# Local transformer on Trainium2: transposing the probabilities one step later, ahead of the feed-forward pieces

## The chip, the cores and the metric

The kernel runs on one core of one Trainium2 chip. The metric is device time in microseconds (us) of one execution. Five engines work side by side, each through its own list of instructions in order: TensorE (PE: matmuls and transposes; PEld is its loading of weights), VectorE (DVE), ScalarE (ACT), GpSimd (POOL), and SyncE (SP), which here only issues DMAs. An engine whose next instruction has to wait lets everything behind it wait too.

## The reference, cut to what matters

The program has two blocks. The part touched here is the second half of block 0: six layers of a local transformer over 16 sequences of 256 tokens with 128 features, in float32.

```python
def attn_layer(x, Wqkv, qs, ksc, Wo):        # 16 heads of 64 features
    q, k, v = split(x @ Wqkv)
    q, k = l2norm(q) * qs, l2norm(k) * ksc
    q, k = rotary(q), rotary(k)              # with rotate_half
    out = local_attention(q, k, v)           # windows of 32 queries, 64 keys: own window and the one before
    return out @ Wo

def ffn_layer(x, g, bln, W1, b1, W2, b2):
    xn = layernorm(x) * g + bln
    a, gate = split(xn @ W1 + b1)
    return a * gelu(gate) @ W2 + b2

for i in range(6):
    x = attn_layer(shift_tokens(x), ...) + x
    x = ffn_layer(shift_tokens(x), ...) + x
```

Before it stands one other attention with its feed-forward, after it a third attention and a last feed-forward; the change touches neither.

## The kernel before

**Tiling.** The 16 sequences are 8 units `u` of two sequences (128 features on the partitions, 512 tokens). The state of a unit lies in `zs[u]`. The 1024 columns of q and k are 8 parts of 128 (two heads each). One step `n` of the main loop takes two parts of one unit; 4 steps (`QS`) are a unit, 32 steps (`per`) a layer, `N` = 192 steps all six layers. "n mod 4" below is the place of a step in this round of four; every unit has one feed-forward, so a round of four steps also holds one feed-forward.

**The pipeline.** All engines but SP are in the order of the program text (`manual_schedule`); the order of SP's DMAs is chosen by the framework's planner. A step works on several stages of different parts at once:

- `project` (step n): q and k of two parts (L705), ACT squares them (L708), DVE makes the two terms of the rotary embedding (L710, L713), four DMAs per part swap halves (`got<-sent`).
- `rotate` (n-1): POOL adds the swapped term (four instructions, L721). `norms_sum` (L729), `norms_inverse` (L747 and small POOL operations) and `norms_rows` (L781) find the inverse norms of two steps at a time, the first two in even steps, the last in odd ones; `widened` fetches them back by DMA (`kn<-rkh`).
- `scaled` (n-4, the head of the step): POOL multiplies k by its norm (two instructions, L802). Then `scores` (L858), `maxima` (DVE, L870 and L872), `exponentials` (ACT, L880: 16 activations, half of them for each of the two parts x), `divided` (DVE reciprocal L893, POOL multiplication L895, once for each x).
- `flipped` (n-5): four transposes (L903) for each x and a copy of the result out of PSUM into `prT`, by ACT for x = 0 (L911), by DVE for x = 1 (L909).
- `weighted` (n-8): the probabilities times the windows of the state (L921), copied into `zx` by DVE and ACT (L934, L936). A unit's first `weighted` needs the last `flipped` of that unit, which stands earlier in the same step.
- `merging` (n-9): `zx` times the merged value and output weights (L942); after four of them `add_to_state` (L955).

`upright` (L809, L813) and `windows` write a unit's state to DRAM and fetch its windows, once or twice per unit.

**The feed-forward** is a generator, `ffn`, in 15 pieces. It is queued in `behind` in the step that ends its unit's `merging`, and `go_on(behind)` runs one piece of it at four places of a step. In this document these are called A (near the head of the step), B (after `weighted`), C (after `norms_inverse`, before `project`) and D (inside `project`). Piece 1 takes the mean (L968) and piece 2 the squares, at C and D of the step that queues it. Piece 3, at A of the next step, sums the squares (L977), takes a power on POOL (`rs`, L987) and widens it on POOL (`fs`, L989). Piece 5, at C of that same step, transposes `fs` (L994) and normalises (L995, L996). Piece 7, at A of the next step, is the gates (L1004) with their gelus on ACT (L1006), piece 11 the other half (L1014, L1018), piece 15 the last product (L1027) with its addition to the state (L957).

**PSUM.** Four banks `mm` go round among all users in program order, three banks `sim` hold scores, one holds `y`. A user of a bank waits until the result of four users before has been copied out.

Of the kernel before, what the change touches and what calls it, by code (L numbers as in the profile page):

```python
# [21 lines left out]
DEPTH = 6  # L22
INNER = 1024
NP = INNER // 128
# [20 lines left out]
def adaln_kernel(  # L45
# [5 lines left out]
    nc = tc.nc  # L51
# [186 lines left out]
    with block:  # L238
# [19 lines left out]
        pt = bank()  # L258
# [341 lines left out]
    with ExitStack() as es:  # L600
# [8 lines left out]
        def atile(tag, shape, bufs=None):  # L609
            kw = {} if bufs is None else {"bufs": bufs}  # L610
            return at.tile(list(shape), F32, tag=tag, name=tag, **kw)
# [166 lines left out]
        def norms_rows(rk):  # L778

            pt = bank()  # L780
            nc.tensor.transpose(pt[0:32, 0:128], rk.rearrange("p t e -> p (t e)"), ident)  # L781
            rows = small("rkT", (32, 128), 2)
            nc.scalar.copy(rows, pt[0:32, 0:128])
            home = dk.tile([8, 4, 128], F32, tag="rkh", name="rkh")
            nc.sync.dma_start(home.rearrange("e t p -> t e p"), rows)
            return home
# [104 lines left out]
        def divided(pr, ssum):  # L891
            rsum = small("rsum", (128, 8))
            nc.vector.reciprocal(rsum, ssum.rearrange("p t h -> p (t h)"))  # L893
            prf = pr.rearrange("p t h k -> p (t h) k")
            nc.gpsimd.tensor_tensor(  # L895
                prf, prf, rsum.unsqueeze(2).to_broadcast([128, 8, 64]), ALU.mult
            )

        def flipped(p, x, pr, prT):

            pt = bank()
            for st in range(4):
                nc.tensor.transpose(  # L903
                    pt[:, st * 128 : (st + 1) * 128],
                    pr[:, x, st].rearrange("p h k -> p (h k)"),
                    ident,
                )
            if x:
                nc.vector.tensor_copy(prT[:, p + x, :], pt)  # L909
            else:  # L910
                nc.scalar.copy(prT[:, p + x, :], pt)  # L911

        def weighted(j, xw, prT):

            zx = atile("zx", (128, 2, NP, 128))
            for k in (2 * j, 2 * j + 1):
                pz = [bank(), bank()]
                for w in range(2):
                    for par in range(2):
                        r = slice(64 * par, 64 * par + 64)  # L920
                        nc.tensor.matmul(  # L921
                            pz[par][:, w * 256 : (w + 1) * 256],
                            xw[r, (2 * k + w) % 8, :],
                            prT[r, :, 64 * k + 32 * w : 64 * k + 32 * w + 32],
                            start=True,
                            stop=True,
                            skip_group_check=True,
                        )
                for par in range(2):
                    c0 = 64 * (k % 2)  # L930
                    dst = zx[:, par, :, c0 : c0 + 64].rearrange("p a (w q) -> p w a q", w=2)
                    src = pz[par].rearrange("p (w a q) -> p w a q", w=2, a=NP)
                    if par:
                        nc.vector.tensor_copy(dst, src)  # L934
                    else:
                        nc.scalar.copy(dst, src)  # L936
            return zx
# [99 lines left out]
        QS = NP // 2  # L1037
        per = NU * QS
        N = DEPTH * per
# [3 lines left out]
        qs, squares, got, prs, prTs = {}, {}, {}, {}, {}  # L1043
# [3 lines left out]
        behind, merges = [], []  # L1047

        def place(n):

            return n // per, n % per // QS, 2 * (n % QS)
# [5 lines left out]
        def go_on(parts):  # L1057
            for g in list(parts):
                if next(g, parts) is parts:
                    parts.remove(g)  # L1060
# [1 line left out]
        es.enter_context(tc.manual_schedule(engines=ENGINES))  # L1062
        merges.append(merged(0))
        n = 0
        while n < N + 9 or behind:
            layer, at_ = divmod(n, per)
            if at_ == 13 and 0 < layer < DEPTH:
                wffs[layer] = load_ffn(layer)
            if 0 <= n - 4 < N:
                for m in (2 * (n - 4), 2 * (n - 4) + 1):  # L1070
                    scaled(m, kns.pop(m))

            w, j = divmod(n - 9, QS)
            if 0 <= w < DEPTH * NU:
                if j == 0:
                    pys[w] = psy.tile([128, 512], F32, tag="y", name="y")
                merging(j, zxs.pop((w, j)), vos[w // NU], pys[w])
                if j == QS - 1:
                    add_to_state(w % NU, pys.pop(w))
            if n % 2 and 3 <= n <= N + 1:  # L1080
                home = norms_rows(rk)
            go_on(behind)
            go_on(merges)
            if 0 <= n - 1 < N:
                for m in (2 * (n - 1), 2 * (n - 1) + 1):
                    rotate(m, qs[m], got.pop(m))
            if 0 <= n - 5 < N:
                i, u, p = place(n - 5)
                if p == 0:
                    prTs[i, u] = atile("prT", (128, NP, 512))  # L1090
                flipped(p, 0, prs[n - 5], prTs[i, u])
            for s, lag in ((0, 7), (1, 9)):
                v, r = divmod(n - lag, QS)
                if r == 0 and 0 <= v < DEPTH * NU:
                    if s == 0:
                        upright(v % NU, rows[v % 2])
                    xws[v, s] = windows(s, rows[v % 2])
            if 0 <= n - 5 < N:
                flipped(p, 1, prs.pop(n - 5), prTs[i, u])
            if 0 <= n - 3 < N:  # L1100
                masked()
            sims = banks[2 * (n - 4) : 2 * (n - 3)] if 0 <= n - 4 < N else None

            if n % 2 == 0 and 2 <= n <= N:
                n2 = norms_sum([squares.pop(m) for m in range(2 * n - 4, 2 * n)])
            v, r = divmod(n - 8, QS)
            if 0 <= v < DEPTH * NU:
                zxs[v, r] = weighted(r, xws[v, r // 2], prTs[v // NU, v % NU])
            go_on(behind)
            if sims:  # L1110
                m = 2 * (n - 4)
                rn = inverses[m // 4][:, m % 4 // 2]
                scores(sims, m, [qs.pop(m), qs.pop(m + 1)])
                pr = atile("pr", (128, 2, 4, 2, 64), 1)
                nbs = [maxima(sims[par], rn[:, par]) for par in range(2)]
                ssum = small("ssum", (128, 2, 4, 2))

            if n % 2 == 0 and 2 <= n <= N:
                rk, inverses[n // 2 - 1] = norms_inverse(n2)
            if 0 <= w < DEPTH * NU and j == QS - 1:  # L1120
                behind.append(ffn(w % NU, w // NU))
            go_on(behind)
            between = exponentials(0, sims, nbs, rn, pr, ssum) if sims else iter(())
            for m in (2 * n, 2 * n + 1):
                if n < N:
                    i, u, p = place(n)
                    qs[m], squares[m], got[m] = project(i, u, m, wqk[p + m % 2], between)
                if m % 2 == 0:
                    go_on(behind)
            if sims:  # L1130
                for x in range(2):
                    for _ in between:
                        pass
                    divided(pr[:, x], ssum[:, x])
                    between = exponentials(1, sims, nbs, rn, pr, ssum) if x == 0 else iter(())
                prs[n - 4] = pr
            if 0 <= n - 3 < N:
                masked()
                for m in (2 * (n - 3), 2 * (n - 3) + 1):
                    kns[m] = widened(m, home)  # L1140
            if layer + 1 < DEPTH:
                if at_ == 18:
                    merges.append(merged(layer + 1))
                if at_ > per - QS:
                    p = 2 * (at_ - (per - QS) - 1)
                    wqk[p : p + 2] = [load_qk(layer + 1, p), load_qk(layer + 1, p + 1)]
            if at_ == 0 and 0 < layer < DEPTH:
                wqk[NP - 2 :] = [load_qk(layer, NP - 2), load_qk(layer, NP - 1)]
            n += 1
# [4 lines left out]
    with ExitStack() as es:  # L1154
# [302 lines left out]
        N = NU * NP  # L1457
# [3 lines left out]
        prs, prTs, oTs, running = {}, {}, {}, []  # L1461
        n = 0
        while n <= N + 4 or running:
            u, p = divmod(n, NP)
            if n < N:
# [4 lines left out]
                sims = [scores(s, q, kT) for s in range(2)]  # L1470
            copies = []
            if 0 <= n - 1 < N:
                u1, p1 = divmod(n - 1, NP)
                g, j = divmod(p1, 4)
# [17 lines left out]
            for lag, g, s in ((6, 0, 0), (7, 0, 1), (9, 1, 0), (10, 1, 1)):  # L1492
                v, r = divmod(n - lag, NP)
# [7 lines left out]
            v, r = divmod(n - 10, NP)  # L1501
# [116 lines left out]
```

## Time and profile before

| | |
|---|---|
| median of 3 runs | 4238.45 us (4237.72 to 4245.77) |
| the profiled execution, its own time | 4247.72 us |
| its span | 4245.9 us |
| TensorE busy | 3844.1 us, 91% of the span |
| DVE, ACT, POOL busy | 2840.9, 2924.1, 2660.5 us (67%, 69%, 63%) |
| mean granted TensorE clock | 0.974 |
| `project` of the first step to that of the last | 268 us to 3540 us after the start of the span |

Busy time of TensorE is time in which at least one matmul is on its way; a granted clock of 1 is full speed, and it is either 1 or 0.5 at any moment. Idle time of an engine that isn't the bound costs nothing. Views used below: the list of waits (engine, line, what it waited for; total us, times, longest us) and the timeline (start in us, duration in us, engine, line, operation, result and inputs, shape, count, and in brackets the idle time before it and what ended it).

### The profile page before, as it was taken

How to read it: one execution, taken by the hardware profiler on the slowest of the kernel's cores; microseconds unless marked ns; L12 is line 12 of the kernel's file. 1: busy time of each engine (PE TensorE's matmuls, PEld its weight loads, DVE VectorE, ACT ScalarE, POOL GpSimd, SP SyncE). 2: the span in 40 equal slices, each digit the busy share in tenths (PEclk: the TensorE clock that was granted, in tenths of full speed). 3: DMA queues.
4: the chain of work that ended last, by engine and by line, in shares of the span. 5: the costliest groups of instructions: out<-in, count | busy, mean ns of one | idle time of the engine just before them, and what ended most of it. 6: DMA issues, size and time to landing. Idle time of an engine off the chain costs nothing.

```text
span 4245.9 us, 117219 instructions
## 1 busy us (share of the span) xinstructions
PE 3844.1 (91%) x44534; PEld 2509.1 (59%) x44534; DVE 2840.9 (67%) x5910; ACT 2924.1 (69%) x9973; POOL 2660.5 (63%) x3374
## 2 busy tenths in 40 slices
PE   7867899999999999999999999999999998799998
PEld 4534666666666666666666666666666666555554
DVE  7745667676766767676766676666667675376664
ACT  4536777777777777777776777777777776366665
POOL 5446666766667676666676666767666665155453
PEclk9888999999999999999999999999999999899999
DMA  1334444444444444454444444444444443200000
GB/s 40 40 90 106 124 114 120 119 113 118 120 114 123 115 114 121 109 129 111 123 117 116 115 117 119 117 120 117 118 107 121 110 120 81 66 1 6 9 4 11
DMA packets 316618, 408.82 MB, mean 96 GB/s; under 512 B 48745, under 2 KB 212632, under 8 KB 316056
## 3 DMA queue, kind: packets, MB, share of 16 engines
q1 hardware_dynamic: 316056, 401.33, 37.8%
q8 instruction: 352, 5.77, 0.6%
q14 instruction: 210, 1.72, 0.1%
HBM read 178.26 MB, written 21.56 MB: 47 GB/s over the span
## 4 chain that ended last, share of the span: by engine, by line
PE 34%; ACT 30%; DVE 14%; issue 7%; POOL 6%; SPq 5%; DMA 4%; ACTq 0%; POOLq 0%; DVEq 0%
ACT pr L880 18%; PE mm L921 8%; PE sim L858 6%; ACT sq L708 6%; PE mm L903 3%; POOL pr L895 3%; PE mm L729 3%; DVE sent L710 3%; DVE mx L870 3%; DMA xw<-rows 3%; PE mm L1396 2%; SPq L793 2%; PE sim L1323 2%; DVE nb L872 2%; PE mm L1386 2%
## 5 line engine op out<-in xcount | busy, mean ns | idle before, releaser
L880 ACT ACTIVATE pr<-sim,nb,rq 128x64 f32<-128x64 f32 x3072 | 1226.6, 448 | 374.0 <-DVE nb L872 362.1
L895 POOL TENSOR_TENSOR pr<-pr,rsum 128x512 f32<-128x512 f32 x384 | 398.6, 1043 | 779.2 <-DVE rsum L893 723.9
L942 PEld LDWEIGHTS y<-zx,wvo 128*128 128x128 f32 x6144 | 715.7, 192 | 91.4 <-issue 88.5
L880 ACT ACTIVATION_READ_ACCUMULATOR pr<-sim,nb,rq 128x1 f32 x3072 | 762.3, 248 | 0.0
L705 PE MATMUL mm<-z,wqk 128*128 128x512 f32 x1536 | 715.7, 605 | 22.8 <-DVE fx L970 12.9
L942 PE MATMUL y<-zx,wvo 128*128 128x128 f32 x6144 | 717.5, 275 | 1.2 <-ACT zx L936 1.2
L710 DVE SCALAR_TENSOR_TENSOR sent<-mm,vec,rope 128x512 f32<-128x512 f32 x768 | 568.5, 740 | 109.8 <-ACT sq L708 101.4
L802 POOL TENSOR_TENSOR k<-k,kn 128x512 f32<-128x512 f32 x384 | 483.4, 1276 | 127.3 <-DMA kn<-rkh 117.5
L721 POOL TENSOR_TENSOR q<-q,got 128x512 f32<-128x512 f32 x384 | 489.1, 1274 | 13.9 <-DMA got<-sent 10.4
L721 POOL TENSOR_TENSOR k<-k,got 128x512 f32<-128x512 f32 x384 | 495.8, 1291 | 0.0
L708 ACT ACTIVATE sq<-mm 128x512 f32<-128x512 f32 x768 | 473.1, 616 | 21.1 <-PE mm L705 20.8
L705 PEld LDWEIGHTS mm<-z,wqk 128*128 128x128 f32 x1536 | 274.6, 191 | 351.0 <-issue 226.1
L934 DVE COPY zx<-mm 128x512 f32<-128x512 f32 x384 | 265.5, 691 | 295.5 <-PE mm L921 295.5
L903 PE MATMUL mm<-ident,pr 128*128 128x128 f32 x1536 | 253.8, 289 | 225.4 <-POOL pr L895 131.1
L921 PE MATMUL mm<-prT,xw 64*128 64x256 f32 x3072 | 424.4, 405 | 5.7 <-DVE zx L934 3.9
L921 PEld LDWEIGHTS mm<-prT,xw 64*128 64x128 f32 x3072 | 321.5, 195 | 127.4 <-issue 55.0
L903 PEld LDWEIGHTS mm<-ident,pr 128*128 128x128 f32 x1536 | 166.1, 144 | 374.0 <-POOL pr L895 358.6
L870 DVE TENSOR_REDUCE mx<-sim 128x8 f32<-128x512 f32 x384 | 263.2, 685 | 173.7 <-PE sim L858 173.6
L936 ACT COPY zx<-mm 128x512 f32<-128x512 f32 x384 | 225.2, 586 | 214.7 <-PE mm L921 214.7
L1366 POOL TENSOR_TENSOR pr<-pr,rsum 128x256 f32<-128x256 f32 (+1 forms) x256 | 205.4, 834 | 244.6 <-DVE rsum L1364 221.0
L858 PEld LDWEIGHTS sim<-k,q 64*32 64x32 f32 x24576 | 264.3, 106 | 90.2 <-issue 42.4
L858 PE MATMUL sim<-k,q 64*32 64x64 f32 x24576 | 300.3, 227 | 18.0 <-POOL k L802 10.6
(254 smaller groups left out, 6386.6 us busy)
## 6 DMA issues: line engine op xcount, KB each, us to landing
got<-sent SPq DMA_DIRECT2D x1536, 128.0 KB
kn<-rkh SPq DMA_DIRECT2D x768, 128.0 KB
xw<-rows SPq DMA_DIRECT2D x384, 128.0 KB
rows<-xt SPq DMA_DIRECT2D x96, 128.0 KB
wqk<-in_L_ffn_Wqkv_dram SPq DMA_DIRECT2D x48, 128.0 KB
bhome<-brow SPq DMA_DIRECT2D x1, 3072.0 KB
wv<-in_L_ffn_Wqkv_dram SPq DMA_DIRECT2D x12, 256.0 KB
wo<-in_L_ffn_Wo_dram SPq DMA_DIRECT2D x12, 256.0 KB
```

The lines of the kernel that those rows point to most:

```text
L705: nc.tensor.matmul(pp, wqk[:, j, :], xs, start=True, stop=True)
L708: nc.scalar.activation(sq, pp, AF.Square)
L710: nc.vector.scalar_tensor_tensor(two(sent[:, j, :]), two(pp), scale, tab[1], ALU.mult, ALU.mult)
L721: nc.gpsimd.tensor_tensor(r, r, two(got[:, j, :]), ALU.add)
L802: nc.gpsimd.tensor_tensor(k, k, two(kn), ALU.mult)
L858: nc.tensor.matmul(sims[par][32 * c : 32 * c + 32, c0 : c0 + 64], q[r, s, t0 : t0 + 32], k[r, s, t0 : t0 + 64], start=False, stop=True, sk ...
L870: nc.vector.tensor_reduce(mx, sim.rearrange("p (b k) -> p b k", b=8), AX.X, ALU.max)
L880: nc.scalar.activation(pr[:, x, st, par, :], sims[par][:, b * 64 : (b + 1) * 64], AF.Exp, bias=nbs[par][:, b : b + 1], scale=rn[:, par, b ...
L895: nc.gpsimd.tensor_tensor(prf, prf, rsum.unsqueeze(2).to_broadcast([128, 8, 64]), ALU.mult)
L903: nc.tensor.transpose(pt[:, st * 128 : (st + 1) * 128], pr[:, x, st].rearrange("p h k -> p (h k)"), ident,)
L921: nc.tensor.matmul(pz[par][:, w * 256 : (w + 1) * 256], xw[r, (2 * k + w) % 8, :], prT[r, :, 64 * k + 32 * w : 64 * k + 32 * w + 32], star ...
L942: nc.tensor.matmul(py[:, j * 128 : (j + 1) * 128], vo[:, h, :], zx[:, h % 2, h // 2, :], start=(h == 0), stop=(h == 2 * NP - 1), skip_grou ...
```

## The change

Six edits, all in the loop of the local transformer:

- The probabilities wait one step longer: `flipped` takes those of n-6 instead of n-5, and `weighted`, `merging`, `upright`, `windows` and the loading of the feed-forward's weights move one step with it. The loop has one step more.
- Both `flipped` of a step stand together; the copy of x = 0 goes from ACT to DVE.
- `rotate`, `flipped`, `upright` and `windows` now stand ahead of place A of the feed-forward, of the pieces of weight merging (`merges`) and of `norms_rows`.
- `divided` of x = 1 moves from the end of its step to the next step, behind the two `flipped` and ahead of place A.
- `pr`, the probabilities, gets two buffers instead of one.
- `zx`, the weighted state, gets one buffer instead of two.

```diff
@@ flipped
-            if x:
-                nc.vector.tensor_copy(prT[:, p + x, :], pt)
-            else:
-                nc.scalar.copy(prT[:, p + x, :], pt)
+            nc.vector.tensor_copy(prT[:, p + x, :], pt)
@@ weighted
-            zx = atile("zx", (128, 2, NP, 128))
+            zx = atile("zx", (128, 2, NP, 128), 1)
@@ the loop
-        while n < N + 9 or behind:
+        while n < N + 10 or behind:
             layer, at_ = divmod(n, per)
-            if at_ == 13 and 0 < layer < DEPTH:
+            if at_ == 14 and 0 < layer < DEPTH:
                 wffs[layer] = load_ffn(layer)
...
-            w, j = divmod(n - 9, QS)
+            w, j = divmod(n - 10, QS)
...
-            if n % 2 and 3 <= n <= N + 1:
-                home = norms_rows(rk)
-            go_on(behind)
-            go_on(merges)
             if 0 <= n - 1 < N:
                 for m in (2 * (n - 1), 2 * (n - 1) + 1):
                     rotate(m, qs[m], got.pop(m))
-            if 0 <= n - 5 < N:
-                i, u, p = place(n - 5)
+            if 0 <= n - 6 < N:
+                i, u, p = place(n - 6)
                 if p == 0:
                     prTs[i, u] = atile("prT", (128, NP, 512))
-                flipped(p, 0, prs[n - 5], prTs[i, u])
-            for s, lag in ((0, 7), (1, 9)):
+                pr = prs.pop(n - 6)
+                for x in range(2):
+                    flipped(p, x, pr, prTs[i, u])
+            if 0 <= n - 5 < N:
+                divided(prs[n - 5][:, 1], ssum[:, 1])
+            for s, lag in ((0, 8), (1, 10)):
                 v, r = divmod(n - lag, QS)
...
-            if 0 <= n - 5 < N:
-                flipped(p, 1, prs.pop(n - 5), prTs[i, u])
+            go_on(behind)
+            go_on(merges)
+            if n % 2 and 3 <= n <= N + 1:
+                home = norms_rows(rk)
...
-            v, r = divmod(n - 8, QS)
+            v, r = divmod(n - 9, QS)
...
-                pr = atile("pr", (128, 2, 4, 2, 64), 1)
+                pr = atile("pr", (128, 2, 4, 2, 64), 2)
...
             if sims:
-                for x in range(2):
-                    for _ in between:
-                        pass
-                    divided(pr[:, x], ssum[:, x])
-                    between = exponentials(1, sims, nbs, rn, pr, ssum) if x == 0 else iter(())
+                for _ in between:
+                    pass
+                divided(pr[:, 0], ssum[:, 0])
+                for _ in exponentials(1, sims, nbs, rn, pr, ssum):
+                    pass
                 prs[n - 4] = pr
```

## The prediction

> **What bounds the kernel now.** The page first: which engine is fullest.
>
> ```profile
> PE 3844.1 (91%) x44534; PEld 2509.1 (59%) x44534; DVE 2840.9 (67%) x5910; ACT 2924.1 (69%) x9973; POOL 2660.5 (63%) x3374
> ```
>
> TensorE. Between 480 and 3560 us it is covered for 2854.71 of 3080 us. Rounds of four steps are 69.1 us long (mean of 41, scores to scores), so TensorE lacks 225.3 / 3080 x 69.1 = 5.05 us a round: all that a better order could win. The list of waits says on what:
>
> ```profile
> PEld mm L903 <- POOL pr L895: 358.6, 312, 6.3
> PE mm L903 <- POOL pr L895: 131.1, 178, 5.5
> PE mm L903 <- ACT fg L1006: 47.2, 46, 2.8
> ```
>
> Mostly the transposes wait for the divided probabilities; `PEld` overlaps matmuls, the `PE` rows are real gaps. Next, TensorE through one step, from scores of an n = 0 (mod 4) step to those of the next:
>
> ```profile
> 2104.97 1.48 PE L858 MATMUL sim<-k,q 64*32 64x64 f32 x128
> ...
> 2106.88 1.02 PE L968 MATMUL mm<-z,mean 128*128 128x512 f32 x2
> 2107.74 2.78 PE L705 MATMUL mm<-z,wqk 128*128 128x512 f32 x6
> 2111.10 1.13 PE L705 MATMUL mm<-z,wqk 128*128 128x512 f32 x2 [0.59 <-DVE fx L970]
> 2112.06 3.73 PE L942 MATMUL y<-zx,wvo 128*128 128x128 f32 x32
> ...
> 2115.74 0.95 PE L977 MATMUL mm<-mean,fs 128*128 128x1 f32 x8
> 2117.70 0.66 PE L903 MATMUL mm<-ident,pr 128*128 128x128 f32 x4 [1.00 <-POOL pr L895]
> 2118.74 0.66 PE L903 MATMUL mm<-ident,pr 128*128 128x128 f32 x4 [0.39 <-POOL pr L895]
> 2119.33 2.00 PE L921 MATMUL mm<-prT,xw 64*128 64x256 f32 x16
> 2121.26 1.58 PE L858 MATMUL sim<-k,q 64*32 64x64 f32 x128
> 2122.86 0.66 PE L994 MATMUL mm<-ident,fs 128*128 128x128 f32 x4
> ```
>
> And POOL at its end:
>
> ```profile
> 2116.60 2.09 POOL L895 TENSOR_TENSOR pr<-pr,rsum 128x512 f32<-128x512 f32 x2 [1.39 <-ACT pr L880]
> 2118.64 2.51 POOL L802 TENSOR_TENSOR k<-k,kn 128x512 f32<-128x512 f32 x2
> 2121.10 1.03 POOL L987 TENSOR_TENSOR rs<-ve,half 128x4 f32<-128x4 f32 x1
> 2122.20 0.61 POOL L989 COPY fs<-rs 128x512 f32<-128x512 f32 x1
> 2122.76 1.27 POOL L721 TENSOR_TENSOR q<-q,got 128x512 f32<-128x512 f32 x1
> ```
>
> POOL ends `fs` at 2122.81 and TensorE transposes it at 2122.86: no slack. `rotate` comes after; the change puts it before.
>
> **What the change removes.** The transposes take probabilities a step older, so their wait goes, and with it the 5.05 us of gaps; what is late next is counted below. ACT loses one 0.59 us copy a step, DVE gains one of 0.69: 0.7 / 17.3 = 4% of a step on an engine 70% busy between 480 and 3560 us, free but for the place named below. The deferred reciprocal makes DVE wait for the last exponential, about 10 us after scores; behind it stand feed-forward pieces and copies of `weighted`, which TensorE first reaches at about 12. The second `pr` buffer is what lets the exponentials run past the later transposes. One `zx` costs nothing: `merging` reads it on TensorE ahead of the `weighted` that fills it again. `norms_rows` (one transpose, one ACT copy of 0.25 us, one small DMA, then four `kn`) comes some 3 us later behind the feed-forward, in n = 3 behind the gelus too; its `kn` is wanted only by the next step's `scaled`, 10 us on. The pieces of weight merging move past POOL work that they don't use, a few times a layer. In SP's queue `rows` and `xw` move to even steps, away from `rkh`. Filling loses a few gaps (5.50, 4.52, 5.08 us) and draining gains one step without scores (about 9 us): taken together as 0, within 10 either way.
>
> **What it adds: `fs` behind `rotate`.** In steps n = 2 (mod 4) POOL now does `scaled`, four `rotate`, the deferred division, then `rs` and `fs`. From the end of scores of the step before:
>
> - DVE's first reciprocal: 9.0. It was 9.8 above (2116.24 - 2106.45) behind norms that this step no longer has, and its median is 8.4 in steps without a feed-forward piece. POOL starts the division 0.36 after the reciprocal's start: 9.4.
> - Division 1.02, `scaled` 2.46, `rotate` 4 x 1.23 = 4.92, division 1.02, `rs` 1.10, `fs` 0.61: done at 20.5.
> - TensorE: mean 0.86, project 3.55 (without its gap), merging 3.57, transposes 2 x 0.60, sums 0.95, norms 1.85 (L729, 2101.10 to 2102.95), weighted 1.93, scores 1.5, inverse 0.5 (2106.38 to 2106.88): at the transposes of `fs` by 15.9.
>
> TensorE stands still 4.6 us, once a round (3.8 to 5.4, by the reciprocal at 8.4 to 9.8). Queued behind it are project, merging and the squares for ACT, so nothing hides it.
>
> **And the clock.** In the loop's filling there are gaps of this size:
>
> ```profile
> 355.02 0.39 PE L781 MATMUL mm<-ident,rk 128*32 128x128 f32 x1 [4.52 <-POOL rk L772]
> 359.83 2.05 PE L858 MATMUL sim<-k,q 64*32 64x64 f32 x128
> 355.00:363.00 8.00, 6.31 (x143) 5.00 (x144) 2.77 (x8) 3.54 (x13) 7.20 (x8) 0.50 0.55 133
> ```
>
> After the gap the granted clock is 0.50 and scores take 2.05 instead of 1.48. All nine gaps of 2.75 us or more in the loop's filling and draining were followed within 5 us by a stretch at half clock, 3.4 to 10.2 us long. Excess over the usual spacing: 2.2 us after 4.52 (transposes 3 x 0.37, scores 0.5, project 0.6), 2.4 after 5.08, 2.1 after 5.50. I take 2.2 (0 to 3.4).
>
> [...]
>
> **Smaller waits that stay.** Steps n = 1: DVE does first reciprocal, `add_to_state` (1.34), two copies (1.32), second reciprocal, and only then the addition of the feed-forward (L957, 1.52), ending near 9.1 + 1.34 + 1.32 + 0.2 + 1.52 = 13.5; `weighted` wants that bank for its third result at 0.5 + 3.55 + 3.57 + 1.2 + 2.7 (L1027) + 0.1 + 1.0 = 12.6: 0.9 (0 to 1.6). It also needs the two copies, done at 11.8, within that time. Steps n = 3: gelus start after the exponentials as before, `weighted` instead of the transposes waits for their banks: 0.4 (0 to 1.0, the old row being 47.2 / 46).
>
> **Sum.** A round: 4.6 + 2.2 + 0.9 + 0.4 = 8.1 us lost against 5.05 now, +3.05. Of 48 feed-forwards 46 fall where project runs: +140 us. The profiled execution (span 4245.9, own time 4247.7) would become 4388; the median of the runs is 9.3 below that execution, so 4238.45 + 140 = 4378. Low ends: (3.8 + 0 - 5.05) x 46 = -58, 4180; high ends: (5.4 + 3.4 + 1.6 + 1.0 - 5.05) x 46 = +292, 4530.
>
> [...]
>
> **Rivals.**
>
> - *The order pays (faster).* Without `fs`'s wait only 0.9 + 0.4 remain: (1.3 - 5.05) x 46 = -172, 4066. It decides where stall and clock together stay below 3.75 us a round, a gap of about 2.5. For it: the rows of waits point at just what is removed. Against: each POOL row of the sum is measured, and 2 us would have to go. 0.18.
> - *The stall comes, the clock holds.* (4.6 + 1.3 - 5.05) x 46 = +39, 4277. Against: nine gaps of nine. 0.12.
> - *Norms come late as well (worse).* SP may put `kn` behind `got`, as it did for three of four in one step of the round before (POOL's `scaled` waited 2.00 us there). With scores about 3 us late once a round: +138 more, 4516. 0.08.
> - *It doesn't do what it says:* another wait holds the transposes and POOL's order moves nothing: 4238. 0.02.
>
> **How the numbers follow.** The forecast, 4378, has 0.60; its own range is 4290 to 4470, from a stall and clock of 4.9 to 8.8 us. Holding 8 in 10 takes in the case with full clock and leaves out the faster rival and most of the worse one: 4225 to 4480. A measurement of this kernel tells about 0.2% (8.5 us) from no change. Faster by more: 0.18. Within it: the last rival and as much from the second's lower edge, 0.04. Slower: the rest, 0.78.
>
> **What would show it.** Right: a row `L994 <- POOL fs L989` of about 46 x 4.6 = 210 us, `L903 <- POOL pr` gone, half-clock stretches in most rounds, n = 2 steps some 6 us longer and the others shorter. Wrong: `fs` done before TensorE needs it, or such gaps at a clock of 1; then a round shrinks toward 65.3 us.

## The result and the profile after

The changed kernel takes 4365.62 us (median of 4 runs, 4360.01 to 4375.79) beside 4242.11 us before (median of 4): 1.0285 times as long, 95% interval 1.0246 to 1.0323. Its profiled execution has a span of 4374.0 us (before 4245.9) and its own time is 4375.79 us. The mean granted clock fell from 0.974 to 0.952.

The page's row of engines, changed kernel:

```profile
PE 3913.8 (89%) x44534; PEld 2566.9 (59%) x44534; DVE 2959.7 (68%) x6102; ACT 2827.4 (65%) x9781; POOL 2642.8 (60%) x3374
```

TensorE has as many instructions as before and is busy 70 us longer: it runs slower somewhere. The list of waits of the changed kernel (total us, times, longest):

```profile
PEld mm L991 <- POOL fs L986: 211.8, 48, 5.0
PE mm L991 <- POOL fs L986: 200.4, 47, 4.8
```

The two rows are its weight-load and matmul side, one gap seen twice. Before, the same wait was:

```profile
PEld mm L994 <- POOL fs L989: 8.5, 31, 2.1
```

The transposes' waits for `pr` are gone from the list. (The lines have moved: L991 and L986 are the transposes of `fs` and `fs` itself, before L994 and L989; L918 is `weighted`, L939 `merging`, L965 and L974 the feed-forward's mean and sums.) TensorE from the scores of an n = 1 step to the project of the n = 2 step, changed kernel:

```profile
2117.76 0.86 PE L858 MATMUL sim<-k,q 64*32 64x64 f32 x64 [0.50 <-POOL k L802]
2118.55 1.13 PE L965 MATMUL mm<-z,mean 128*128 128x512 f32 x2
2119.51 3.67 PE L705 MATMUL mm<-z,wqk 128*128 128x512 f32 x8
...
2126.59 1.04 PE L903 MATMUL mm<-ident,pr 128*128 128x128 f32 x8
...
2132.13 1.59 PE L858 MATMUL sim<-k,q 64*32 64x64 f32 x128
2133.64 0.66 PE L747 MATMUL mm<-ident,n 128*128 128x128 f32 x4
2138.88 1.12 PE L991 MATMUL mm<-ident,fs 128*128 128x128 f32 x4 [4.58 <-POOL fs L986]
2139.79 5.30 PE L705 MATMUL mm<-z,wqk 128*128 128x512 f32 x8
```

The eight transposes (L903) now run without a gap; then TensorE stands for 4.58 us, and the project behind it takes 5.30 us where the one of the step before took 3.67. POOL in the same stretch:

```profile
2127.75 1.04 POOL L895 TENSOR_TENSOR pr<-pr,rsum 128x512 f32<-128x512 f32 x1 [4.13 <-PE mm L903]
2128.75 2.51 POOL L802 TENSOR_TENSOR k<-k,kn 128x512 f32<-128x512 f32 x2
2131.21 1.28 POOL L721 TENSOR_TENSOR q<-q,got 128x512 f32<-128x512 f32 x1
...
2136.12 1.05 POOL L895 TENSOR_TENSOR pr<-pr,rsum 128x512 f32<-128x512 f32 x1
2137.12 1.03 POOL L984 TENSOR_TENSOR rs<-ve,half 128x4 f32<-128x4 f32 x1
2138.21 0.61 POOL L986 COPY fs<-rs 128x512 f32<-128x512 f32 x1
```

(The view puts the first division's wait down to the transposes, which ended last before it; the reciprocal that it reads had begun at 2127.38.) POOL is never idle from this division on: `scaled`, `rotate`, the deferred division, and only then `rs` and `fs`, which ends 20.2 us after the scores (2138.82 - 2118.62). The windows view (length, busy times, granted clock third from the end) shows the clock over the gap and over what follows it:

```profile
2134.30:2138.90 4.60, 0.02 (x1) 0.03 (x1) 2.82 (x6) 0.88 (x4) 4.54 (x6) 0.73 0.02 8
2138.90:2145.00 6.10, 6.10 (x13) 3.07 (x14) 3.62 (x6) 2.97 (x11) 3.68 (x13) 0.65 0.00 0
```

The clock is halved already inside the gap (0.73 over 4.60 us), where TensorE has nothing to do, and stays so for some 4 us of the work behind it (0.65 over 6.10 us). Between 480 and 3560 us it is at half for 240 us, before for 27 us.

### The profile page after: what moved, and what is told of

The parts are those of the page before. It is cut to its first block, busy times and chain, and to the rows that moved or that the text cites. A ratio compares the mean times of both kernels' runs of the same rounds, so it can differ in the third digit from the quotient of the medians.

```text
span 4374.0 us, 117288 instructions
## 1 busy us (share of the span) xinstructions
PE 3913.8 (89%) x44534; PEld 2566.9 (59%) x44534; DVE 2959.7 (68%) x6102; ACT 2827.4 (65%) x9781; POOL 2642.8 (60%) x3374
## 4 chain that ended last, share of the span: by engine, by line
PE 44%; DVE 16%; POOL 12%; ACT 9%; DMA 7%; issue 7%; SPq 5%; POOLq 0%; ACTq 0%; DVEq 0%
PE mm L705 7%; PE mm L918 5%; PE y L939 5%; DVE sent L710 5%; PE sim L858 4%; ACT pr L880 4%; DMA kn<-rkh 3%; PE mm L1011 3%; POOL k L721 3%; DMA got<-sent 2%; PE mm L729 2%; DVE q L713 2%; DVE k L713 2%; PE mm L1001 2%; POOL k L802 2%
## 5 line engine op out<-in xcount | busy, mean ns | idle before, releaser
L705 PE MATMUL mm<-z,wqk 128*128 128x512 f32 x1536 | 789.9, 661 | 10.7 <-DMA wqk<-in_L_ffn_Wqkv_dram 7.6
L939 PEld LDWEIGHTS y<-zx,wvo 128*128 128x128 f32 x6144 | 715.8, 192 | 91.7 <-issue 88.3
L939 PE MATMUL y<-zx,wvo 128*128 128x128 f32 x6144 | 717.9, 275 | 1.5 <-ACT zx L933 1.5
L705 PEld LDWEIGHTS mm<-z,wqk 128*128 128x128 f32 x1536 | 315.3, 216 | 379.5 <-issue 295.5
L918 PE MATMUL mm<-prT,xw 64*128 64x256 f32 x3072 | 443.8, 396 | 18.0 <-ACT sim L844 2.3
L918 PEld LDWEIGHTS mm<-prT,xw 64*128 64x128 f32 x3072 | 319.3, 187 | 194.1 <-issue 45.1
L1351 ACT ACTIVATE pr<-lg,nm 128x128 f32<-128x128 f32 (+1 forms) x512 | 226.3, 443 | 119.8 <-DVE nm L1340 109.4
L713 DVE SCALAR_TENSOR_TENSOR q<-mm,vec,rope 128x512 f32<-128x512 f32 x384 | 284.7, 742 | 0.0
```

Of the source, the lines that this page charges most:

```text
L705: nc.tensor.matmul(pp, wqk[:, j, :], xs, start=True, stop=True)
L713: nc.vector.scalar_tensor_tensor(r, two(pp), scale, tab[0], ALU.mult, ALU.mult)
L918: nc.tensor.matmul(pz[par][:, w * 256 : (w + 1) * 256], xw[r, (2 * k + w) % 8, :], prT[r, :, 64 * k + 32 * w : 64 * k + 32 * w + 32], star ...
L939: nc.tensor.matmul(py[:, j * 128 : (j + 1) * 128], vo[:, h, :], zx[:, h % 2, h // 2, :], start=(h == 0), stop=(h == 2 * NP - 1), skip_grou ...
```

## The experiments

**Theory:** POOL's order puts `fs` behind `rotate`, TensorE waits for it, and its clock is halved afterwards. **Rivals:** the loss comes from another part of the change (the longer pipeline, the DVE copies, the late norms), and the wait for `fs` only collects it; or project is slow after the gap for another reason than the clock.

### POOL's order alone, undone

```diff
-            if 0 <= n - 1 < N:
-                for m in (2 * (n - 1), 2 * (n - 1) + 1):
-                    rotate(m, qs[m], got.pop(m))
...
             go_on(behind)
+            if 0 <= n - 1 < N:
+                for m in (2 * (n - 1), 2 * (n - 1) + 1):
+                    rotate(m, qs[m], got.pop(m))
             go_on(merges)
```

> The changed kernel with rotate moved behind place A of the feed-forward: only POOL's order differs (and what SP's planner makes of it). Theory (fs stands behind rotate on POOL, TensorE waits, and its clock is halved after the wait): the gap of 4.45 us a round and the 1.8 us of half clock go, 46 x 6.3 = 290 us less than the changed kernel's 4366, so about 4080; granted clock back at 0.97. Rival (the loss lies in the longer pipeline, the DVE copies or the late norms, and the wait for fs only collects it): TensorE waits elsewhere for about as long, 4300 to 4370.

Measured: 4107.5 us (4101.1 to 4117.52), 0.9657 of before (0.9634 to 0.968). TensorE, DVE and ACT have the changed kernel's order; four POOL instructions stand elsewhere (and SP's queue differs in a few places). TensorE at the same place:

```profile
2127.43 0.66 PE L747 MATMUL mm<-ident,n 128*128 128x128 f32 x4
2127.92 0.60 PE L991 MATMUL mm<-ident,fs 128*128 128x128 f32 x4
2128.36 3.07 PE L705 MATMUL mm<-z,wqk 128*128 128x512 f32 x6
```

No gap, no slow clock (0.98 over the run). 258 us of the 290 expected went; part of the rest is a new wait, 0.49 us a round, of `project` for the normalisation (L992). So the order of `rotate` and `fs` costs more than the whole loss of the change, and the rest of the change is a gain of 3.4%.

### The same order in the kernel before

```diff
+            if 0 <= n - 1 < N:
+                for m in (2 * (n - 1), 2 * (n - 1) + 1):
+                    rotate(m, qs[m], got.pop(m))
             go_on(behind)
             go_on(merges)
-            if 0 <= n - 1 < N:
-                for m in (2 * (n - 1), 2 * (n - 1) + 1):
-                    rotate(m, qs[m], got.pop(m))
```

> The kernel before with one edit: rotate ahead of place A. Theory: the wait for fs arises by itself, 4.5 us and 1.8 us of half clock a round (there in steps n = 1), 46 x 6.3 = 290 us more than 4242: about 4530, and the old waits of the transposes stay. Rival (the old waits of the transposes and the new one are two faces of one delay and share it): about 4242 to 4400.

Measured: 4485.75 us (4481.76 to 4487.04), 1.0543 of before (1.0525 to 1.056). Its TensorE:

```profile
2106.07 1.12 PE L994 MATMUL mm<-ident,fs 128*128 128x128 f32 x4 [5.02 <-POOL fs L989]
2106.98 4.52 PE L705 MATMUL mm<-z,wqk 128*128 128x512 f32 x8
```

Moving four POOL instructions makes the gap and the half clock (0.956 over the run, 0.974 before) by itself, without any other part of the change. It cost 231 us beside the before of the same runs (4255.11), not 290. The wait for `fs` came out as expected, 4.52 us a round (mean of 42), but the wait of the next step's transposes for the gelus' banks vanished (0.99 us a round before), with 0.6 us put down to POOL's `scaled` in its place: a small part of the old delay is shared.

### The gap filled with matmuls

```diff
+            filler = bank()
+            for _ in range(9):
+                nc.tensor.matmul(filler, mean128, xn, start=True, stop=True)
             rb = bank()
```

> The changed kernel with nine matmuls of 128x512, whose result nobody reads, in the gap ahead of the transposes of fs (about 4.0 us of work in a gap of 4.45). Theory (part of the loss is half clock after the gap): the clock holds, project takes 3.6 us again in steps n = 2, 46 x 1.8 = 83 us less, about 4283, although TensorE has more work. Rival (project is slow there for another reason, such as waits for banks or DVE): 4366 or, with work that doesn't fit the gap, up to 40 us more.

Measured: 4476.56 us (4472.2 to 4482.2), 1.0527 of before. This run was badly sized: one such matmul is two instructions of 0.44 us, so the filler took 7.89 us in a gap of 4.5 and the time tells nothing for or against. The trace does: project after the filler takes 3.60 us, and the clock is 0.981. With four matmuls instead of nine:

> As the run with nine unread matmuls, whose 7.89 us were almost twice the gap (each is two instructions of 0.44 us), with four: 3.5 us of work in a gap of 4.45. Theory: the clock holds at 0.98, project takes 3.6 us again, 46 x 1.8 = 83 us less than the changed kernel's 4366: about 4283. Rival: the half clock isn't what makes project slow, or comes for another reason: 4366.

Measured: 4303.75 us (4299.2 to 4308.49), 1.0142 of before (1.0128 to 1.0157), 62 us below the changed kernel although TensorE has 3.6 us more work a round:

```profile
2166.23 3.60 PE L991 MATMUL mm<-fx,mean 128*128 128x512 f32 x8
2170.67 0.66 PE L994 MATMUL mm<-ident,fs 128*128 128x128 f32 x4 [0.84 <-POOL fs L986]
2171.16 3.60 PE L705 MATMUL mm<-z,wqk 128*128 128x512 f32 x8
```

`fs` is as late as before, but the gap is 0.84 us, the clock is 0.98 over the run, where the changed kernel has 0.952 and half clock 45 times between 480 and 3500 us, and project is back at 3.60 us. Rounds shrink by 1.60 us (72.27 to 70.67). This is the price of the clock by itself, or a little less than it: `weighted` now waits 0.32 us a round for the gelus' banks (0.02 in the changed kernel), which may come of the bank that the filler takes. The other rival falls.

### The feed-forward ahead again

```diff
+            go_on(behind)
             if 0 <= n - 1 < N:
...
                     xws[v, s] = windows(s, rows[v % 2])
-            go_on(behind)
             go_on(merges)
```

> The changed kernel with place A of the feed-forward back ahead of rotate and of the transposes on all engines (norms_rows and weight merging stay where the change put them). Theory: fs is in time, so about 4080, within 30 us of the kernel that moves rotate alone; in steps n = 3 the transposes wait for the gelus' banks again, in steps n = 0 the second half of the feed-forward waits longer for project's banks. Rival (having the transposes ahead of the feed-forward is worth something itself): 40 us or more above the kernel that moves rotate alone.

Measured: 4152.68 us (4144.14 to 4154.98), 0.9758 of before (0.9739 to 0.9776). `fs` is in time, so the theory's main part holds, but this is 45 us above the kernel that moves `rotate` alone, beyond the 30 it allowed: the order of transposes and feed-forward is worth something itself. Of the round's additional 0.9 us, the n = 1 steps hold most: `weighted` waits 1.75 us there, and 0.12 where the transposes stand first. With the feed-forward ahead, the copies of the transposes, which a unit's first `weighted` needs in that very step, stand on DVE behind the addition of the feed-forward's output (L954), and `weighted` starts when they end:

```profile
2068.85 1.52 DVE L954 SCALAR_TENSOR_TENSOR z<-mm,vec,z 64x512 f32<-64x512 f32 x2 [0.58 <-PE mm L1024]
2070.40 1.29 DVE L908 COPY prT<-mm 128x512 f32<-128x512 f32 x2
2071.79 2.09 PE L918 MATMUL mm<-prT,xw 64*128 64x256 f32 x16 [1.99 <-issue]
```

No run took that addition alone away. The clock is a little lower as well: 0.99 between 480 and 3400 us and 0.973 over the run, where `rotate` alone moved has 1.00 and 0.98. Of the smaller waits that the theory named, that of the transposes in steps n = 3 came (0.26 us a round), that of the second half of the feed-forward in steps n = 0 did not.

### The division of x = 1 in its own step

```diff
-            if 0 <= n - 5 < N:
-                divided(prs[n - 5][:, 1], ssum[:, 1])
...
                 for _ in exponentials(1, sims, nbs, rn, pr, ssum):
                     pass
+                divided(pr[:, 1], ssum[:, 1])
```

> The kernel that moves rotate behind the feed-forward, with the division of x = 1 back at the end of its own step (ahead of scaled on POOL, its reciprocal ahead of the copies on DVE). Theory: the reciprocal makes DVE's copies wait for the last exponential, so weighted waits about 1.7 us in steps n = 1 and the feed-forward 1 us in steps n = 0, and scaled comes 1.5 us later: 70 to 180 us more, about 4225. Rival (only the age of the probabilities matters, not where they are divided): 4107.

The base is the kernel with `rotate` behind the feed-forward, 0.9657 of its own before. Measured: 4247.73 us (4245.07 to 4261.18), 1.0015 of before (1.0003 to 1.0027): 140 us above its base, or 152 if each is set beside its own before. Its waits:

```profile
PEld mm L918 <- DVE prT L908: 102.3, 89, 3.6
PEld mm L1011 <- DVE prT L908: 86.8, 46, 1.9
```

The reciprocal stands ahead of the copies on DVE, waits for the last exponential, and the copies come late for `weighted` (0.82 us a round) and for the second half of the feed-forward (1.09). All that the corrected kernel gains over before is lost without the deferral: here the transposes' greater age paid only while nothing else on DVE waited for ACT ahead of their copies.

### The copy of x = 0 on ACT, and one buffer of zx

```diff
-            nc.vector.tensor_copy(prT[:, p + x, :], pt)
+            if x:
+                nc.vector.tensor_copy(prT[:, p + x, :], pt)
+            else:
+                nc.scalar.copy(prT[:, p + x, :], pt)
```

> The kernel that moves rotate behind the feed-forward, with the copy of x = 0 back on ACT. Theory: on DVE the copy is done before the last exponential, on ACT only after it, and in steps n = 0 the second half of the feed-forward waits about 0.5 us for that bank: 23 us more, 4130 (0 to 60 more). Rival (DVE, with 2 copies, is what TensorE waits for in steps n = 0): up to 30 us less, 4080.

Measured: 4120.95 us (4115.11 to 4125.22), 0.9715 of before (0.9699 to 0.973), 13 us above its base, or 25 if each is set beside its own before: DVE is the better place, by about the 23 us expected. The second half of the feed-forward waits 0.29 us a round more in steps n = 0, where 0.5 was expected.

```diff
-            zx = atile("zx", (128, 2, NP, 128))
+            zx = atile("zx", (128, 2, NP, 128), 1)
```

> The kernel before with one buffer of zx. Theory: merging reads it on TensorE ahead of the weighted that fills it again, so nothing waits: the time of before within 8 us. Rival (the copies into zx wait for merging): 0.2 us or more a step, 40 us or more.

This one is the kernel before with that edit alone. Measured: 4242.32 us, 0.9999 of before (0.9987 to 1.0011). The buffer was spare.

### Four buffers of kn

```diff
-            kn = atile("kn", (128, 512))
+            kn = atile("kn", (128, 512), 4)
```

> The kernel that moves rotate behind the feed-forward, with four buffers of kn instead of two. In it scaled of steps n = 1 waits 2.97 us for the second kn, whose two DMAs stand behind got in SP's queue because the buffer is free only after scaled of the step before, and scores wait 0.65 us a round for it. Theory: with four buffers the planner puts them ahead of got, 46 x 0.65 = 30 us less than 4107: about 4077. Rival (the scores would next wait for something else, or SP's queue only shifts): 4100 to 4115.

Measured: 4262.95 us (4251.1 to 4283.49), 1.0033 of before (1.002 to 1.0047): 155 us slower than its base (160 each beside its own before) instead of 30 faster. The 0.65 us did go (0.02 a round left). But SP's planner used its freedom in the next step. SP and POOL there:

```profile
2152.22 0.93 SPq L716 DMA_DIRECT2D got<-sent  x1
2153.19 2.51 SPq L793 DMA_DIRECT2D kn<-rkh  x4
```

```profile
2157.12 1.26 POOL L802 TENSOR_TENSOR k<-k,kn 128x512 f32<-128x512 f32 x1 [4.80 <-DMA kn<-rkh]
2158.94 1.27 POOL L802 TENSOR_TENSOR k<-k,kn 128x512 f32<-128x512 f32 x1 [0.56 <-DMA kn<-rkh]
```

The `kn` that the n = 2 step needs is issued behind all of `got`, although its source, `rkh`, had been sent off at 2134.90 (the base issues these `kn` 2.2 us after `rkh`); `scaled` waits 4.80 us for it, the scores 2.51 us a round; the project behind it takes 4.89 us, and the clock is 0.958 over the run, where the base has 0.98. The only edit is the number of buffers, the other four engines' order is the same, so the loss is SP's order. Fixing that order by hand wasn't tried.

## Why the prediction was right

The prediction was 4378 us, range 4225 to 4480, slower at 0.78; measured 4365.62.

- **The stall.** Predicted from the end of scores: division at 9.4, `fs` done at 20.5, TensorE there at 15.9, 4.6 us. In the round shown: 9.1, 20.2, 15.7 (2134.30) and 4.58 us; mean 4.38. The sum of POOL rows behind the reciprocal was right term by term. Undoing that order alone turned 1.0285 into 0.9657, doing it alone gave 1.0543.
- **The clock.** Predicted 2.2 us a round from gaps in the loop's filling; measured 1.60 by filling the gap (up to 1.9 if the filler's own wait is added). Half clock came as predicted, the term was 0.3 to 0.6 too large. Project was the only large matmul block in the slow stretch, 5.30 - 3.6 = 1.7 us; the gaps of the filling had three blocks behind them.
- **Half clock after the gap.** The prediction took it from nine gaps of 2.75 us or more in the filling and draining before, all followed by half clock. Between 480 and 3660 us the changed kernel has 44 gaps of 3 to 5 us, and each was followed by half clock of 3.4 or 6.8 us.
- **The smaller waits** were placed wrongly and summed 0.6 too small. n = 1 steps: 0.9 predicted, 0.13 found. n = 3 steps: 0.4 predicted, 0.02 found. Instead 1.15 us a round fall in n = 0 steps, where `upright` and the second half of the feed-forward reach project's banks before DVE has emptied them (0.46 and 0.69), and 0.63 us in the scores of n = 1 steps, which wait for `scaled` and late `kn`. 1.3 predicted, 1.93 found. This error and that of the clock's term have opposite signs and nearly cancel: that the sum came so close is in part luck. The wait for late `kn` is the worse rival in small, the whole of which the run with four `kn` buffers shows.
- **The count of rounds and the ends.** A round grew by 3.17 us (69.10 to 72.27, mean of 42), predicted 3.05. Over these 42 rounds, step 16 to 184, the two kernels differ by 133 us; what stands before them became 7 us shorter, and the last steps with the draining cost 2 more. Taking 46 rounds and 0 for the ends gave 140 where the spans differ by 128: the 42 rounds were put at 128 and gave 133, the rest was put at 12 (four rounds more) and gave -5.
- **The faster rival** had the right mechanism at the wrong size of one term: without `fs`'s wait the gaps fall to 2.84 us a round and not 1.3, and the kernel takes 4107.5 and not 4066.

## What to carry to other kernels

When a step is moved in the program text, go through every engine's queue that it passes, also those on which it looks cheap: here four additions on POOL, an engine at 63%, passed two instructions of 1.7 us that TensorE needed at once. A group that TensorE waits for should stand as early on its engine as its inputs allow, and a change that takes away waits should be read with its worst new wait undone before it is judged; this one was worth 3.4% under a loss of 2.9%. An added buffer is also a freedom for whoever orders the transfers, and isn't safe to give without looking at the queue it produces.

## What the runs showed of the hardware

Between 480 and 3660 us, TensorE's clock was at half after every gap above 2.5 us in the kernel before and in the changed one, and after some shorter gaps. Counted there, with half clock that begins in the gap or within 5 us behind it: in the changed kernel all 44 gaps of 3 to 5 us (3.31 to 4.78), four of five between 1.6 and 2.5 us (1.66, 1.87, 1.89 and 2.22 us; the one of 1.88 us was followed by none), and none of 124 between 0.3 and 1.6 us; in the kernel before both gaps above 2.5 us (2.79 and 3.25), all five between 1.6 and 2.5 us, and ten of 178 between 0.8 and 1.2 us (some gaps there stand close together, so a single one may owe its stretch to its neighbour). The shortest stretch at half clock was 3.4 us long in both.

And filling a gap with matmuls that nobody reads paid here: 3.6 us of useless work a round made the changed kernel 62 us faster, with the clock back from 0.952 to 0.98.
